# The front of a macaron block: loading all sequences of x at once, issuing the stores of x after those of the rows, and giving the experts' search its own SBUF places

## The chip, the core and the metric

The kernel runs on one core of a Trainium2 chip. The metric is the device time of one execution in microseconds (us). The median of three runs before the change is 5663.02 us (5660.18 to 5664.28). The profile is of one further execution.

Names used below: PE is TensorE's matmul, PEld its weight load, DVE is VectorE, ACT is ScalarE, POOL is GpSimd, SP is the engine whose queue issues most DMAs. L181 is line 181 of the kernel before the change.

## The reference, cut to what matters

The input x has 8 sequences of 1024 tokens of 256 float32 numbers. The network is two "layers": a half-weighted mixture of experts, causal attention, the same mixture again, then a channel mix, a state-space block and the channel mix again. Only the mixture bears on this change:

```python
def _L0_ffn_ref(x, Wr, br, W_up, b_up, W_down, b_down):
    ...
    k = n_tok // E                       # 8192 tokens, 8 experts: 1024 each
    xf = x.reshape(n_tok, h)
    logits = xf @ Wr + br
    Sm = jax.nn.softmax(logits, axis=-1)
    G_t, idx_t = jax.lax.top_k(Sm.T, k)  # each expert takes its 1024 best tokens
    ...
    y = jnp.zeros_like(xf).at[idx].add(G[..., None] * out)
...
x = L0_attn_x
x = x + 0.5 * _L0_ffn_ref(_layernorm(x, axis=-1), ...)
x = x + _L0_attn_ref(_layernorm(x, axis=-1), ...)
x = x + 0.5 * _L0_ffn_ref(_layernorm(x, axis=-1), ...)
```

An expert picks tokens among all 8192, so no expert can start before the probabilities of all eight sequences are known.

## The kernel before, in words

Nearly all data are float32, laid on 128 partitions. A sequence is a tile of 128 x 8 x 256: 8 pieces of 128 tokens. DRAM holds `acc` (x plus what is added to it) and `rows` (for each token its 256 normalised numbers and 8 probabilities). One SBUF tile `S` holds all probabilities.

**The front** (the loop at the start of `tile_macaron_kernel`, L1800 to L1804) does for each sequence b: load x into `xt` (L1802, 1024 KB, SP queue), `moe.front` (below), and store `xt` to `acc[0]` (L1804, 1024 KB, SP queue). The pool "f" has two buffers of each of its tiles, `xt` among them. Tile's scheduler orders the instructions of this loop itself: it is not under `tc.manual_schedule()`, within which each engine keeps the order in which the program wrote its instructions.

`steps_front` (L164 on) is a generator; `front` runs it through. For one sequence its steps are:

1. `normalise`: DVE takes the statistics (L75 x8, L77 x8), ACT the square root (L79), DVE the reciprocal (L81) and the normalised copy `moe_r` (L88 x8).
2. Four steps, each with four PE transposes (L177) of two pieces, and one ACT copy from PSUM into `moe_xT` (L181).
3. The logits: 16 matmuls, which the profile records as 32 with a weight load each (L186), and a DVE add of the bias (L191).
4. Maximum, subtraction (DVE, L196, L197) and exponential (ACT, L200).
5. Sum, reciprocal, product into `moe_r`, copy into `S` (DVE, L203 to L210), and the store of `moe_r` into `rows` (L213, 1056 KB, SP queue).

The square root and the exponential are in different ACT tables; a change between them puts an ACT_TABLE_LOAD ahead.

**The search** (`choose`, L217 on) transposes `S` (L227, L231), finds each expert's threshold in 30 rounds of DVE, PE, DVE (L249, L236, L254 to L262), and turns the chosen places into two tiles `lo` and `hi` (L300, L301). Its `full` tile is set by a POOL memset (L279).

**The experts** (`run`, under `tc.manual_schedule()`): POOL memsets of the weights' and middle tiles (L363 to L374), SP loads of the weights of the first two experts (`load(0)`, `load(1)`, L383 to L399), then the search in pools opened inside `run`, then for each expert a list of tokens (`steps_list`, L310 to L344), a gather of their rows (POOL, L428), the matmuls (L462, L479) and a scatter that adds into `acc` (POOL, L487).

`run` is called twice: after the front, and after the attention stage, whose own generator `steps_front` writes `S` and `rows[1]` (store at L908). Ahead of the second call, `Layer1` loads and prepares the weights of the second half (L1061 to L1116).

Of the kernel before, what the change touches and what calls it, by code (L numbers as in the profile page):

```python
# [8 lines left out]
F32 = mybir.dt.float32  # L9
# [5 lines left out]
PSUM = bass.MemoryType.PSUM  # L15
DRAM = bass.MemoryType.DRAM

P = 128
D = 256
# [3 lines left out]
E = 8  # L23
# [81 lines left out]
class Moe:  # L105
# [6 lines left out]
    def __init__(self, cp, net, Wr, br, W_up, b_up, W_down, b_down):  # L112
        self.net, nc = net, net.nc
        self.W_up, self.b_up, self.W_down, self.b_down = W_up, b_up, W_down, b_down
        C, KT = net.C, net.KT
        self.SC = C // self.SP
        assert self.SC * E == P
        self.wr = cp.tile([P, KC, E], F32, name="wr")
        nc.sync.dma_start(self.wr, Wr.rearrange("(k p) e -> p k e", p=P))
        self.br = cp.tile([P, E], F32, name="br")  # L120
        nc.sync.dma_start(self.br, br.partition_broadcast(P))

        one = cp.tile([P, E], F32, name="of_e")
        nc.vector.tensor_reduce(
            one, net.ident.rearrange("p (c e) -> p e c", e=E), AX.X, ALU.add
        )
        self.same = cp.tile([P, self.SC, E], F32, name="same")
        nc.vector.tensor_copy(self.same, one.unsqueeze(1).to_broadcast([P, self.SC, E]))
        self.same = self.same.rearrange("p c e -> p (c e)")
        self.before = cp.tile([P, P], F32, name="before")  # L130
        nc.gpsimd.affine_select(
            self.before, self.same, [[1, P]], ALU.is_gt, 0.0, base=0, channel_multiplier=-1
        )

        ii = cp.tile([P, P], I32, name="ii")
        nc.gpsimd.iota(ii, [[1, P]], base=0, channel_multiplier=0)
        self.col = cp.tile([P, P], F32, name="col")
        nc.vector.tensor_copy(self.col, ii)
        ip = cp.tile([P, 1], I32, name="ip")
        nc.gpsimd.iota(ip, [[0, 1]], base=0, channel_multiplier=1)  # L140
        self.row = cp.tile([P, 1], F32, name="row")
        nc.vector.tensor_copy(self.row, ip)
        ic = cp.tile([P, self.SP, self.SC], I32, name="ic")
        nc.gpsimd.iota(ic, [[1, self.SP], [self.SP, self.SC]], base=0, channel_multiplier=0)
        self.cno = cp.tile([P, self.SP, self.SC], F32, name="cno")
        nc.vector.tensor_copy(self.cno, ic)

        self.join = cp.tile([P, KT], F32, name="join")
        parts = net.ident.rearrange("p (g j) -> p j g", j=32)
        hi = cp.tile([P, KT], F32, name="join_hi")  # L150
        nc.vector.tensor_reduce(hi, parts[:, 0:KT, :], AX.X, ALU.add)
        nc.vector.tensor_reduce(self.join, parts[:, KT : 2 * KT, :], AX.X, ALU.add)
        nc.vector.scalar_tensor_tensor(self.join, hi, float(P), self.join, ALU.mult, ALU.add)
# [149 lines left out]
    def steps_list(self, e, lo, hi, wh, idx, two, ps):  # L303
# [39 lines left out]
        nc.tensor.matmul(pi, sums, self.join, start=True, stop=True)  # L343
        nc.vector.tensor_copy(idx, pi)  # L344

    def run(self, S, rows, acc):

        net, nc, tc = self.net, self.net.nc, self.net.tc
# [3 lines left out]
        with ExitStack() as st:  # L352
            def pool_in(name, bufs, **kw):
                return st.enter_context(tc.tile_pool(name=name, bufs=bufs, **kw))
# [4 lines left out]
            wp = pool_in("ex_w", 1)  # L359
# [17 lines left out]
            def load(e):  # L377
# [22 lines left out]

            load(0)
            load(1)
            lo, hi = (
                wp.tile([P, self.SP, self.SC, E], F32, name=name) for name in ("lo", "hi")
            )
            with tc.tile_pool(name="ch", bufs=1) as pool, tc.tile_pool(
                name="ch2", bufs=2
            ) as two, tc.tile_pool(name="ch_ps", bufs=2, space=PSUM) as ps:
                self.choose(S, lo, hi, pool, two, ps)
            tp, mp = pool_in("ex_t", 2 * KT), pool_in("ex_m", 2)  # L410
            op, ip, two = pool_in("ex_o", 4), pool_in("ex_i", 3), pool_in("ex_2", 2)
            pst, psm, pso = (
# [1328 lines left out]
def kernel(  # L1741
# [30 lines left out]
    nc = tc.nc  # L1772
    B, T, _ = x.shape
    net = Net(ctx, tc, B, T)
    N, NT = net.N, net.NT
# [3 lines left out]
    moe = Moe(mcp, net, Wr, br, W_up, b_up, W_down, b_down)  # L1779
    S = moe.probabilities(mcp)  # L1780
# [3 lines left out]
    acc = [dram1.tile([N, D], F32, name=f"acc{i}") for i in range(2)]  # L1784
    rows = [dram1.tile([N, ROW], F32, name=f"rows{i}") for i in range(2)]

    def of(a, b):

        return a[b * T : (b + 1) * T, :].rearrange("(c p) d -> p c d", p=P)

    def pool_in(st, name, bufs, **kw):
        return st.enter_context(tc.tile_pool(name=name, bufs=bufs, **kw))

    xf, of_out = x.rearrange("b t d -> (b t) d"), out.rearrange("b t d -> (b t) d")
    with ExitStack() as st:
        at = Attention(net, pool_in(st, "at_w", 1), w_qkv, w_out, b_out)
        with ExitStack() as ph:
            pool = pool_in(ph, "f", 2)
            ps = pool_in(ph, "f_ps", 3, space=PSUM)
            for b in range(B):  # L1800
                xt = pool.tile([P, NT, D], F32, name="xt")
                nc.sync.dma_start(xt, of(xf, b))  # L1802
                moe.front(pool, ps, xt, b, rows[0], S, "mm")
                nc.sync.dma_start(of(acc[0], b), xt)  # L1804
        with tc.manual_schedule():
            moe.run(S, rows[0], acc[0])
        with ExitStack() as ph:
            at.places(pool_in(ph, "at_qk", 1), dram1)
            pools = {
                name: pool_in(ph, f"at_{name}", bufs) for name, bufs in (  # L1810
                    ("x", 3), ("xn", 2), ("xT", 1), ("side", 1), ("pT", 4), ("so", 2), ("oT", 2),
                    ("over", 2), ("sm", 2), ("junk", 1), ("r", 1), ("rT", 1),
                )
            }
            for name, banks in (("s1", 3), ("s2", 3), ("po", 1), ("mm", 1)):
                pools[name] = pool_in(ph, f"at_{name}", banks, space=PSUM)

            pools["dram"] = dram2

            def load(xt, b):  # L1820
                nc.sync.dma_start(xt, of(acc[0], b))

            def store(xt, b):
                nc.sync.dma_start(of(acc[1], b), xt)
                yield from at.steps_front(moe, xt, b, rows[1], S)

            with tc.manual_schedule():
                at.run(pools, load, store)
    with ExitStack() as st:
        w = pool_in(st, "l1_w", 1)  # L1830
        layer1 = Layer1(
            net, w, Wr_t, Wk_t, Wv_t, mu_r, mu_k, ln_gamma, ln_beta, in_proj_t, conv_w, conv_b,
            x_proj_t, dt_proj_t, dt_proj_b, A_log, Dp, out_proj_t,
        )
        with tc.manual_schedule():
            moe.run(S, rows[1], acc[1])
        of_moe.close()
        pools = {
            name: pool_in(st, f"l1_{name}", bufs) for name, bufs in (
                ("x", 2), ("mixT", 1), ("ka", 2), ("r", 2), ("hT", 2), ("u", 1), ("uc", 2 * NDC),  # L1840
                ("xd", 1), ("delta", 1), ("du", 1), ("sp1", 1), ("zs", 1),
                ("rep", 1), ("sdl", 3), ("sdu", 3), ("dbu", 2), ("hc", 6), ("tap", 1), ("through", 1), ("xn", 2), ("small", 2),
            )
        }
        pools["dram"] = dram2
        pools["ps"] = pool_in(st, "l1_ps", 2, space=PSUM)
        pools["y"] = pool_in(st, "l1_y", 1, space=PSUM)
        pools["h"] = pool_in(st, "l1_h", 2, space=PSUM)

        def load(xt, b):  # L1850
            nc.sync.dma_start(xt, of(acc[1], b))

        def store(xt, b):
            nc.sync.dma_start(of(of_out, b), xt)

        def load_x(xt, b):
            nc.sync.dma_start(xt, of(acc[0], b))

        def keep_x(xt, b):
            nc.sync.dma_start(of(acc[0], b), xt)  # L1860

        with tc.manual_schedule():
            layer1.run(pools, load, load_x, keep_x, store)
# [39 lines left out]
```

## Time and profile before

| what | value |
|---|---|
| median of three runs | 5663.02 us |
| the profiled execution, its own time | 5670.78 us |
| its span, first to last instruction | 5668.9 us |
| PE busy | 4660.3 us (82%) |
| DVE busy | 3431.4 us (61%) |
| ACT busy | 2505.6 us (44%) |
| POOL busy | 2205.0 us (39%) |
| mean granted TensorE clock | 0.890 |
| last copy into S of the front begins | 129.05 us |
| first expert's list begins (L310) | 199.70 us |
| first expert matmul (L462, weight load) | 228.8 us |
| last copy into S ahead of the second search begins | 2294.17 us |
| second search begins (L227) | 2302.19 us |

In a row of the timeline stand: start, duration, engine, line, operation, tile written <- tiles read, shapes, how often, and in brackets how long its engine was idle before and what ended that. In a row of stretches stand: the stretch and its length, the busy time and number of instructions of PE, PEld, DVE, ACT and POOL, then the granted TensorE clock (1.00 is full), the mean busy share of the DMA engines, and the GB/s that they moved. SPq rows are DMAs as SP issues them. The profile has one execution; positions in it are us from the span's start.

### The profile page before, as it was taken

Reading aid. Unit: us, or ns where it says so; the run is one execution under the profiler, and the core shown is the slowest. Engines: PE = TensorE matmul, PEld = TensorE weight load, DVE = VectorE, ACT = ScalarE, POOL = GpSimd, SP = SyncE. Lnnn points to the kernel's source line nnn. Section 1 sums busy time; section 2 is a strip of 40 time slices with the busy share of each in tenths; the row PEclk is TensorE's granted clock in tenths of the full one; section 3 lists DMA queues with packets and bytes.
Section 4 is the critical chain, followed back from the end, with each engine's and each line's share of the span. In section 5 each row is a group of like instructions: output and inputs, shape, how many; then the busy total and the mean of one; then the engine's idle time right before and its main releaser. Section 6 shows DMA issues by size and latency. Waiting matters only on the chain.

```text
span 5668.9 us, 60303 instructions
## 1 busy us (share of the span) xinstructions
PE 4660.3 (82%) x21302; PEld 2227.0 (39%) x21302; DVE 3431.4 (61%) x5653; ACT 2505.6 (44%) x4152; POOL 2205.0 (39%) x1801
## 2 busy tenths in 40 slices
PE   5599699999999998399776778788787778878867
PEld 5355434444444443255532233333333324333324
DVE  4532166667666762633107877777767777677884
ACT  2011145666565553011144645465464645546443
POOL 1244201111111110234316656556555666556662
PEclk7699889999999997599887889889898888989888
DMA  6123312122221220223206454535536463454652
GB/s 201 33 57 60 79 37 75 58 74 68 81 74 59 77 69 27 68 49 62 44 13 156 134 145 122 153 98 143 138 105 158 110 163 108 112 153 114 169 137 63
DMA packets 252976, 545.28 MB, mean 96 GB/s; under 512 B 29681, under 2 KB 143681, under 8 KB 252674
## 3 DMA queue, kind: packets, MB, share of 16 engines
q1 hardware_dynamic: 228098, 507.34, 32.1%
q0 software_dynamic: 24576, 34.10, 3.7%
q8 instruction: 168, 2.75, 0.2%
q14 instruction: 134, 1.10, 0.1%
HBM read 400.31 MB, written 141.03 MB: 95 GB/s over the span
## 4 chain that ended last, share of the span: by engine, by line
PE 25%; DVE 13%; ACT 6%; issue 5%; DMA 2%; POOL 1%; SPq 0%; DVEq 0%; POOLq 0%; ACTq 0%
DVE h L1719 8%; PE y L1647 5%; PE pc L1366 4%; PE pr L1261 4%; PE pk L1239 4%; PE pu L1417 2%; DVE hc L1724 2%; PE pp L1501 2%; ACT h L1625 2%; PE pd L1432 1%; ACT xn L1195 1%; PE px L1396 1%; DMA sdu<-du 1%; DVE ln_st L1182 1%; ACT L1131 1%
## 5 line engine op out<-in xcount | busy, mean ns | idle before, releaser
L767 ACT ACTIVATE pT<-s 128x512 f32<-128x512 f32 (+3 forms) x1536 | 670.7, 488 | 554.9 <-PE s L724 546.7
L1625 ACT ACTIVATE h<-sdl,A 128x1024 f32<-128x1024 f32 x512 | 567.0, 1112 | 644.4 <-DVE hc L1724 622.4
L724 PE MATMUL s<-kT,qT 32*128 32x512 f32 (+3 forms) x3072 | 839.5, 540 | 12.9 <-DVE mx L740 8.0
L1647 PE MATMUL y<-hc,pick 128*32 128x512 f32 x2048 | 648.5, 714 | 227.6 <-DVE hc L1724 227.6
L724 PE MATMUL s<-qT,kT 32*128 32x512 f32 (+3 forms) x3072 | 763.7, 547 | 13.3 <-ACT pT L767 13.3
L1616 POOL TENSOR_TENSOR dbu<-sdu,b 128x1024 f32<-128x1024 f32 x256 | 602.3, 2353 | 405.3 <-DMA sdu<-du 217.5
L1719 DVE TENSOR_TENSOR_SCAN h<-h,dbu 128x1024 f32<-128x1024 f32 x256 | 586.1, 2289 | 184.4 <-ACT h L1625 159.8
L1719 DVE TENSOR_TENSOR_SCAN h<-h,sdu 128x1024 f32<-128x1024 f32 x256 | 586.2, 2290 | 160.6 <-ACT h L1625 146.3
L1724 DVE TENSOR_TENSOR hc<-h,c 128x1024 f32<-128x1024 f32 x512 | 625.6, 1222 | 30.4 <-PE y L1647 2.5
L773 POOL TENSOR_SCALAR_AFFINE_SELECT pT<-pT 128x512 f32<-128x512 f32 x256 | 162.4, 634 | 1180.7 <-ACT pT L767 1097.2
L1616 POOL TENSOR_TENSOR sdu<-sdu,b 128x1024 f32<-128x1024 f32 x256 | 602.4, 2353 | 14.4 <-DMA b<-bc 3.7
L724 PEld LDWEIGHTS s<-kT,qT 32*128 32x128 f32 x3072 | 327.6, 187 | 437.1 <-DVE mx L740 184.6
L466 ACT ACTIVATE mid<-pm,bu 128x512 f32<-128x512 f32 x192 | 131.6, 686 | 734.3 <-PE pm L462 734.3
L737 DVE TENSOR_REDUCE part<-s 128x1 f32<-128x512 f32 x512 | 329.7, 685 | 187.1 <-PE s L724 186.5
L487 POOL DMA_INDIRECT acc<-o,idx x128 | 211.2, 1650 | 502.0 <-DVE o L484 229.7
L1647 PEld LDWEIGHTS y<-hc,pick 128*32 128x32 f32 x2048 | 126.7, 125 | 712.0 <-issue 391.4
L740 DVE CUSTOM_DVE_ANT_0 junk<-s,mask,part 128x256 f32<-128x256 f32 (+3 forms) x512 | 281.5, 550 | 159.7 <-PE s L724 114.7
L462 PE MATMUL pm<-tT,wu 128*128 128x512 f32 x768 | 364.0, 612 | 0.0
L479 PE MATMUL po<-wd,mid 128*128 128x256 f32 x1536 | 352.0, 393 | 0.0
L787 PE MATMUL po<-pT,at_v 128*32 128x512 f32 (+3 forms) x3072 | 337.1, 512 | 0.3 <-POOL pT L773 0.3
L740 DVE CUSTOM_DVE_ANT_0 junk<-s,mask 128x256 f32<-128x256 f32 (+3 forms) x512 | 250.4, 489 | 136.5 <-PE s L724 84.9
L479 PEld LDWEIGHTS po<-wd,mid 128*128 128x128 f32 x1536 | 305.1, 200 | 44.3 <-issue 1.0
(262 smaller groups left out, 6736.8 us busy)
## 6 DMA issues: line engine op xcount, KB each, us to landing
sdl<-dl SPq DMA_DIRECT2D x256, 512.0 KB
sdu<-du SPq DMA_DIRECT2D x256, 512.0 KB
acc<-xt SPq DMA_DIRECT2D x24, 1024.0 KB
xt<-acc SPq DMA_DIRECT2D x24, 1024.0 KB
rows<-moe_r SPq DMA_DIRECT2D x16, 1056.0 KB
qT<-padded_q SPq DMA_DIRECT2D x32, 512.0 KB
kT<-padded_k SPq DMA_DIRECT2D x32, 512.0 KB
kept<-so SPq DMA_DIRECT2D x64, 256.0 KB
```

What stands on the lines that cost most here:

```text
L462: nc.tensor.matmul(pm, wu[:, k, n * P : (n + 1) * P], tT[:, k, t0 : t0 + HALF], start=(k == 0), stop=(k == KC - 1),)
L479: nc.tensor.matmul(po, mid[:, n, j * P : (j + 1) * P], wd[:, n, :], start=(n == 0), stop=(n == NF - 1),)
L724: self.net.nc.tensor.matmul(s[:, 0 : rhs.shape[-1]], lhsT, rhs, start=True, stop=True)
L737: nc.vector.tensor_reduce(part, sh, AX.X, ALU.max)
L740: nc.vector.tensor_tensor_reduce(junk[:, 0:w], sh[:, 0:w], self.mask[:, W - w : W], 1.0, part if a else -3e38, ALU.add, ALU.max, self.mx[n ...
L767: self.net.nc.scalar.activation(pT[:, h, 0:w], sh[:, 0:w], AF.Exp, scale=1.0 / HD**0.5)
L787: nc.tensor.matmul(q.po[h * HS : (h + 1) * HS, o:W], self.va[q.b % 2][:, j, g * HG + h, :], pT[:, h, 0 : W - o], start=(j == 0), stop=(j = ...
L1616: nc.gpsimd.tensor_tensor(inputs[i], t, seqs[b].rep["b", p], ALU.mult)
L1625: nc.scalar.activation(decays[i], spread["dl", i - p], AF.Exp, scale=self.A[:, p, n : n + 1])
L1647: nc.tensor.matmul(self.py[g * self.RG : (g + 1) * self.RG, t0 : t0 + W], self.pick[:, j, :], hc[:, t0 : t0 + W], start=False, stop=(j == ...
L1719: nc.vector.tensor_tensor_scan(decays[i], decays[i], inputs.pop(i), 0.0, ALU.mult, ALU.add)
L1724: nc.vector.tensor_tensor(hc, decays.pop(i), seqs[b].rep["c", p], ALU.mult)
```

## The change

There are four edits.

- Front: the eight tiles `xt` have a pool of their own with eight buffers, and all eight loads are issued first. The sequences are then worked through by a list of at most two generators of `steps_front`. A new one is admitted where the turn number is divisible by four and fewer than two are under way; in each turn every generator advances one step. With nine calls to a generator (eight steps and its end), sequence 0 starts in turn 0, sequence 1 in turn 4, sequence 2 in turn 12, sequence 3 in turn 16, and so on. When a generator ends, `xt` is stored to `acc[0]`, one turn after the store of its rows. All of it is under `tc.manual_schedule()`.
- `lo` and `hi` move from a pool of `run` to the pool of the experts' constants, which lies at the right side of SBUF.
- The search gets pools at the right side of SBUF (`room`), opened ahead of the front's pools, and a PSUM pool of its own (`chosen`).
- The search is called before `run` and not in it, for both layers; in `run`, loads and memsets are therefore behind it in the order of the program.

```diff
+        self.lo, self.hi = (
+            cp.tile([P, self.SP, self.SC, E], F32, name=name) for name in ("lo", "hi")
+        )
...
+    def room(self, st):
+
+        st = st.enter_context
+        return (
+            st(self.net.tc.tile_pool(name="ch", bufs=1, side="right")),
+            st(self.net.tc.tile_pool(name="ch2", bufs=2, side="right")),
+        )
+
+    def chosen(self, S, room):
+
+        with self.net.tc.tile_pool(name="ch_ps", bufs=2, space=PSUM) as ps:
+            self.choose(S, self.lo, self.hi, *room, ps)
...
             load(0)
             load(1)
-            lo, hi = (
-                wp.tile([P, self.SP, self.SC, E], F32, name=name) for name in ("lo", "hi")
-            )
-            with tc.tile_pool(name="ch", bufs=1) as pool, tc.tile_pool(
-                name="ch2", bufs=2
-            ) as two, tc.tile_pool(name="ch_ps", bufs=2, space=PSUM) as ps:
-                self.choose(S, lo, hi, pool, two, ps)
+            lo, hi = self.lo, self.hi
...
-        with ExitStack() as ph:
-            pool = pool_in(ph, "f", 2)
-            ps = pool_in(ph, "f_ps", 3, space=PSUM)
-            for b in range(B):
-                xt = pool.tile([P, NT, D], F32, name="xt")
-                nc.sync.dma_start(xt, of(xf, b))
-                moe.front(pool, ps, xt, b, rows[0], S, "mm")
-                nc.sync.dma_start(of(acc[0], b), xt)
+        with ExitStack() as ro:
+            room = moe.room(ro)
+            with ExitStack() as ph, tc.manual_schedule():
+                pool, px = pool_in(ph, "f", 2), pool_in(ph, "f_x", B)
+                ps = pool_in(ph, "f_ps", 3, space=PSUM)
+                xs = []
+                for b in range(B):
+                    xs.append(px.tile([P, NT, D], F32, name="xt"))
+                    nc.sync.dma_start(xs[b], of(xf, b))
+
+                todo, works = list(range(B)), []
+                turn = 0
+                while todo or works:
+                    if todo and len(works) < 2 and turn % 4 == 0:
+                        b = todo.pop(0)
+                        works.append((b, moe.steps_front(pool, ps, xs[b], b, rows[0], S, "mm")))
+                    turn += 1
+                    for b, steps in list(works):
+                        if next(steps, 0) == 0:
+                            works.remove((b, steps))
+                            nc.sync.dma_start(of(acc[0], b), xs[b])
+            with tc.manual_schedule():
+                moe.chosen(S, room)
         with tc.manual_schedule():
             moe.run(S, rows[0], acc[0])
...
         with tc.manual_schedule():
+            with ExitStack() as ro:
+                moe.chosen(S, moe.room(ro))
             moe.run(S, rows[1], acc[1])
```

## The prediction

> **What bounds the kernel here.** The page's chain of waits, asked for 0 to 700 us, has no piece there, so it does not say what the front is worth. I therefore read three stretches, cut where the trace changes its work: to the end of the last copy into S (129.05 + 0.20), to the first expert's list (199.70), to the first expert matmuls.
>
> ```profile
> 0.00:129.25 129.25, 77.22 (x384) 74.84 (x384) 59.87 (x265) 36.48 (x59) 10.92 (x22) 0.83 0.61 198
> 129.25:199.70 70.45, 21.53 (x74) 18.00 (x74) 43.81 (x170) 0.00 (x0) 8.68 (x11) 0.50 0.18 55
> 199.70:230.00 30.30, 12.48 (x150) 7.77 (x151) 25.34 (x31) 0.00 (x0) 13.79 (x11) 0.50 0.16 43
> ```
>
> In the front no engine is full: PE 77 of 129 us, DVE 60, ACT 36, DMA 0.61 of its time. It is bound by waits between them. The search (70.45 us) is a chain of DVE and PE in turn, and it starts from the last S. From 240 us on PE is busy 58.98 of 60 us. So a microsecond gained before the last S is gained one for one, and the change's other parts must be found between 129 and 230 us and at the second search.
>
> Next the timeline of the front, the rows that set its pace:
>
> ```profile
> 18.25 3.70 PE L177 MATMUL tr_moe<-ident,moe_r 128*128 128x128 f32 x16 [18.25 <-DVE moe_r L88]
> 21.74 6.84 PE L186 MATMUL moe_pl<-wr,moe_xT 128*128 128x8 f32 x32
> 28.43 3.85 PE L177 MATMUL tr_moe<-ident,moe_r 128*128 128x128 f32 x16
> 32.24 7.00 PE L186 MATMUL moe_pl<-wr,moe_xT 128*128 128x8 f32 x32
> ...
> 67.76 0.20 DVE L210 COPY S<-moe_r 128x64 f32<-128x64 f32 x1
> 67.87 2.71 DVE L75 BATCH_NORM_STATS2 ln_st<-xt 128x6 f32<-128x256 f32 x8
> ...
> 71.19 1.28 ACT L79 ACT_TABLE_LOAD   x1 [4.22 <-DVE ln_mv L77]
> ...
> 73.62 3.70 PE L177 MATMUL tr_moe<-ident,moe_r 128*128 128x128 f32 x16 [7.76 <-DVE moe_r L88]
> ...
> 77.11 4.12 PE L186 MATMUL moe_pl<-wr,moe_xT 128*128 128x8 f32 x32
> ```
>
> Sequences 0 and 1 form one PE block, 18.25 to 39.24 (20.99 us). The whole front is such blocks and gaps: blocks of 20.99, 20.24 (45.61 to 65.85), 7.61 (73.62 to 81.23), 21.04 (90.44 to 111.48) and 7.36 us (118.50 to 125.86), in sum 77.24; gaps between them of 6.37, 7.77, 9.21 and 7.02, in sum 30.37; 18.25 ahead and 3.39 behind. Sum 129.25, the measured end.
>
> Two rows stand out: the 32 logits instructions take 6.84 to 7.00 us in the blocks of two, but 4.12 (77.11) and 3.88 (121.98) in the lone ones. The stretches around them, cut every 3.41 us, show why:
>
> ```profile
> 74.68:78.09 3.41, 3.41 (x19) 3.41 (x17) 1.05 (x4) 2.34 (x4) 0.00 (x0) 1.00 1.03 322
> 78.09:81.50 3.41, 3.14 (x28) 3.04 (x27) 0.23 (x1) 0.00 (x0) 0.00 (x0) 1.00 1.04 335
> 81.50:84.90 3.40, 0.00 (x0) 0.00 (x0) 1.61 (x8) 2.79 (x3) 0.00 (x0) 0.50 0.03 8
> 119.08:122.49 3.41, 3.41 (x19) 3.41 (x17) 1.53 (x5) 2.02 (x4) 0.00 (x0) 0.50 0.54 179
> 122.49:125.90 3.41, 3.38 (x30) 3.29 (x30) 0.00 (x0) 0.33 (x1) 0.00 (x0) 1.00 0.00 0
> ```
>
> The clock goes from 0.50 to 1.00 at 122.49 and back at 125.90. (Up to the first fall at 81.5 the column says 1.00 throughout, but the durations show half clock; I go by the durations.) The step comes after a window that the 3.7 us of transposes fill wholly or mostly; 78.09 and 122.49 lie 13 x 3.415 us apart, so the windows seem to run on a fixed grid. At 18.25 or 90.44 the transposes straddle two windows, and the logits stay slow. So six sequences ran at half clock, two at full clock, and whether a sequence is lucky hangs on its start against a grid that this kernel doesn't set.
>
> **Loads at once.** Eight loads stand at the head of SP's queue; two of them took 1.06 us to issue, so six more take about 3.2 us of an SP that otherwise waits until 12 us. Sequence 0 landed at 12.19 (first statistics), sequence 1 at about 15.15 (SP's wait for it, the shorter of two, 2.6 us after 12.56): one after the other, 3.0 us apart. By this the last lands at 12.2 + 7 x 3.0 = 33 us, and is needed past 100. What goes: SP's waits at L1802, 18.3 us for the store of x and 14.0 for DVE. But they are not four times on the path, since what is late next is the chain of the pair itself.
>
> **The new order.** By the turns, sequences 0/1, 2/3, 4/5, 6/7 form pairs: the second starts with the first's last transposes, and the first of the next pair is written behind the S copy of the pair before. On DVE that is a strict order: S copy, then statistics. The trace has this handover at 65.85: logits end, S copy ends at 67.96, statistics at 67.87, table load, transposes at 73.62, a gap of 7.77 us. Inside a pair, the second's normalisation lies under the first's logits: in the pair at 18.25, DVE would end it by 17.3 + 2.7 + 2.7 + 0.6 + 0.6 + 2.7 = 26.6, before 28.43, so the block stays 21.0 us. The sum, all at half clock: first transposes at 18.09 (the reciprocal no longer stands behind six statistics of the next sequence, 17.15 for 17.31), four blocks of 21.02 = 84.06, three gaps of 7.77 = 23.31, and 2.11 behind the last logits (65.85 to 67.96; no table load, the pair's first exponential did it). That is 127.57, against 129.25: 1.7 us less.
>
> So the gaps fall by 7.06 us, the tail by 1.28 and the start by 0.16, but the blocks grow by 6.82, most of which is the two lucky sequences (6.95 - 4.12 and 6.95 - 3.88: 2.83 + 3.07 = 5.9). Bounds for luck: none of eight, or six or so of eight (2.4 us of transposes in one window were enough at 74.68, 2.2 us at 91.77 were not; so by an estimate from these, about 2 of the 3.41 us of the grid are lucky starts). I take two of eight as in this trace: 127.6 - 5.9 = 121.7, a gain of **7.5 us**. The lucky span is one window, so 2.9 us each.
>
> [...]
>
> **Stores.** A row store landed 4.8 us after issue (129.05; the wait at L383 ended 133.87). `moe_r` has two buffers; sequence 0's store goes out near 32.8 and its buffer is written again near 46.5, 13.7 us later, so nothing waits. Per pair of 28.8 us the stores are 4.3 MB, 150 GB/s where 12 to 18 us shows 368. The last x store is now behind the last rows: about 3 us more until the experts' weights and memsets may enter those places. They took 8.4 us (134.04 to 142.43) and are needed at 200.4 (wh) and 228.8 (wu), so 57 us of search hide them; uncovered they would cost those 8.4.
>
> **The search's places.** Before, the transposes of S began 0.11 us after the copy ended (129.36): no wait goes. At the second search PE's row at 2302.19 was released by ACT's A (L1115), whose chain begins with the load of A_log, issued at 2295.20 and landed at 2301.16. That stays. If the new places lie over `moe_r`, whose store was issued at 2294.16, the first write (2303.35) would wait for it; the DMAs were at 1.02 up to 2300 and at 0.19 after, so it had landed 3 us before. Zero. POOL's `full` (0.52 us) moves ahead of the memsets and is needed 60 us later: zero.
>
> **The sum** against the profiled execution: 5670.8 - 7.5 = 5663.3. The median of the runs is 7.8 us below that execution, so I put the same difference on it: 5663.0 - 7.5 = 5655.5.
>
> **Rivals.**
> - Forecast, one to three lucky sequences: -4.6 to -10.4, so 5652.6 to 5658.4. Chance 0.48.
> - The gaps shrink but no sequence is lucky: -1.7, 5661.3. For it: six of eight before were not. Chance 0.20. [...]
> - Four or more lucky: five give -1.7 - 14.7 = -16.4, 5646.6. The three table loads in the gaps could add 3 x 1.28 if they went out early, as the one at 83.65 did. For it: four pairs start after 7.8 idle us, as both lucky ones did. Chance 0.24.
> - Slower: the eight loads share the DMA engines evenly, and sequence 0 lands with the last at 33 us, not at 12.2. That is 20.8 later for the whole front: -7.5 + 20.8 = +13.3, 5676.3. It loses as soon as sequence 0 lands later than 19.7. Against it: sequences 0 and 1 landed 3 us apart though issued together. Chance 0.08.
>
> A measurement of this kernel can tell about 0.2%, 11.3 us, from no change. The first two cases lie within it (0.68), the third is faster (0.24), the fourth slower (0.08). The range reaches from six lucky ones and part of the table loads (-22) to the second case and a few us of shift further on (+4): 5641 to 5667; it leaves out the fourth case and the tail of the third.
>
> **What would show it.** Right: eight loads in a row on SP from 3.3; first transposes near 18.1 and, of the third sequence, near 46.9; three gaps near 7.8; the last S between 117 and 128; the list 70.4 us behind it. Wrong: sequence 0 not landed by 13; a PE wait inside a pair; a wait for a row store at L88; a second search later than 8 us behind its last S.

## The result, and the profile after

The changed kernel took 5650.92 us (median of 14 runs, 5634.01 to 5662.78) against 5662.1 us (14 runs, 5639.07 to 5671.88). The ratio is 0.9975 with a 95% interval of 0.9965 to 0.9985: 0.25% faster, about 14 us, 8 to 20 by the interval. The profiled execution took 5638.44 us with a span of 5636.2.

| position or length, us | before | after |
|---|---|---|
| first transposes of the front | 18.25 | 17.96 |
| last copy into S ends | 129.25 | 109.25 |
| first expert's list begins | 199.70 | 179.64 |
| search, last S to list | 70.45 | 70.39 |
| first expert matmul to first attention exponential | 527.2 | 519.2 |
| second search's first transpose behind its last S copy's start | 8.0 | 8.0 |
| span | 5668.9 | 5636.2 |

The same stretches as before the change (stretch, length, busy time of PE, PEld, DVE, ACT, POOL with counts, clock, DMA share, GB/s):

```profile
0.00:109.25 109.25, 65.51 (x384) 62.43 (x384) 62.14 (x265) 33.50 (x57) 11.33 (x23) 0.69 0.67 221
109.25:179.60 70.35, 21.48 (x74) 17.95 (x74) 43.77 (x170) 0.00 (x0) 8.21 (x10) 0.50 0.25 77
```

The front is 20 us shorter with the same 384 PE instructions. PE itself was busy 11.7 us less (65.51 for 77.22): less idle time is only part of it, the same instructions also ran faster. The search kept its length. The front's PE rows:

```profile
17.96 3.69 PE L180 MATMUL tr_moe<-ident,moe_r 128*128 128x128 f32 x16 [17.96 <-DVE moe_r L88]
21.44 3.73 PE L189 MATMUL moe_pl<-wr,moe_xT 128*128 128x8 f32 x32
25.03 3.59 PE L180 MATMUL tr_moe<-ident,moe_r 128*128 128x128 f32 x16
28.84 4.39 PE L189 MATMUL moe_pl<-wr,moe_xT 128*128 128x8 f32 x32 [0.23 <-ACT moe_xT L184]
...
63.52 3.69 PE L180 MATMUL tr_moe<-ident,moe_r 128*128 128x128 f32 x16 [7.77 <-DVE moe_r L88]
67.01 6.83 PE L189 MATMUL moe_pl<-wr,moe_xT 128*128 128x8 f32 x32
73.70 3.79 PE L180 MATMUL tr_moe<-ident,moe_r 128*128 128x128 f32 x16
77.56 6.99 PE L189 MATMUL moe_pl<-wr,moe_xT 128*128 128x8 f32 x32
92.33 3.69 PE L180 MATMUL tr_moe<-ident,moe_r 128*128 128x128 f32 x16 [7.77 <-DVE moe_r L88]
95.81 4.01 PE L189 MATMUL moe_pl<-wr,moe_xT 128*128 128x8 f32 x32
```

Six of the eight sequences have their 32 logits instructions in 3.7 to 4.4 us, the pair at 63.52 alone in 6.8 to 7.0. The gaps ahead of pairs are 7.71, 7.77 and 7.77 us (41.2 us of PE's waits for `moe_r` with the first one's 18.0). Cut along the grid of 3.413 us that the clock's steps give (here its falls at 24.91 and 106.83 lie 24 x 3.413 us apart):

```profile
18.09:21.50 3.41, 3.41 (x17) 3.33 (x18) 3.41 (x12) 1.76 (x3) 0.00 (x0) 1.00 1.10 348
21.50:24.92 3.42, 3.42 (x33) 3.42 (x33) 3.01 (x17) 0.89 (x2) 0.00 (x0) 1.00 1.10 348
24.92:28.33 3.41, 3.41 (x17) 3.18 (x17) 2.17 (x8) 2.14 (x4) 0.00 (x0) 0.50 1.11 350
28.33:31.74 3.41, 3.18 (x29) 2.94 (x27) 0.84 (x4) 1.43 (x3) 0.00 (x0) 1.00 1.09 347
...
62.46:65.87 3.41, 2.35 (x11) 2.30 (x12) 3.11 (x10) 1.14 (x3) 0.00 (x0) 0.50 0.89 298
65.87:69.29 3.42, 3.42 (x19) 3.42 (x17) 2.99 (x17) 1.73 (x4) 0.00 (x0) 0.50 0.02 5
```

PE is fully busy in each of the first three. After the window of transposes (18.09) the next is fast, with 33 instructions in it; after that window of logits the clock is 0.50 again. At 62.46 only 2.35 us are transposes, and the window after it stays at 0.50. (Up to the first fall, at 24.9 here, the column says 1.00 whatever the durations say.)

SP's rows, one execution of the changed kernel:

```profile
3.30 21.00 SPq L1815 DMA_DIRECT2D xt<-in_L_attn_x_dram  x8
...
109.05 0.36 SPq L216 DMA_DIRECT2D rows<-moe_r  x1
109.45 0.76 SPq L1827 DMA_DIRECT2D acc<-xt  x1
117.54 0.37 SPq L399 DMA_DIRECT2D wu<-in_L_ffn_W_up_dram  x1
```

The eight loads held SP for 21 us, and nothing was due on SP before 29.09. The experts' weights entered the front's places at 117.54, 8.3 us behind the last S.

### The profile page after: what moved, and what is told of

It reads as the page before. It is cut to its first block, busy times and chain, and to the rows that moved or that the text cites. A ratio compares the mean times of both kernels' runs of the same rounds, so it can differ in the third digit from the quotient of the medians.

```text
span 5636.2 us, 60291 instructions
## 1 busy us (share of the span) xinstructions
PE 4643.4 (82%) x21302; PEld 2203.4 (39%) x21302; DVE 3432.4 (61%) x5653; ACT 2503.6 (44%) x4150; POOL 2204.0 (39%) x1801
## 4 chain that ended last, share of the span: by engine, by line
PE 26%; DVE 13%; ACT 6%; issue 5%; DMA 2%; POOL 1%; SPq 0%; DVEq 0%; POOLq 0%; ACTq 0%
DVE h L1729 8%; PE y L1657 5%; PE pc L1376 4%; PE pr L1271 4%; PE pk L1249 4%; PE pu L1427 2%; DVE hc L1734 2%; PE pp L1511 2%; ACT h L1635 2%; PE pd L1442 1%; PE pm L472 1%; ACT xn L1205 1%; PE px L1406 1%; DMA sdu<-du 1%; PE po L489 1%
## 5 line engine op out<-in xcount | busy, mean ns | idle before, releaser
L476 ACT ACTIVATE mid<-pm,bu 128x512 f32<-128x512 f32 x192 | 131.6, 686 | 722.2 <-PE pm L472 722.2
```

## The experiments

The theory at their start (A): the new order of the pairs and the PE clock set the front's length, the early loads are cover. Rivals: the early loads are the gain (B); the search's places are (C); the fast logits have another cause than the transposes' windows (D). All kernels compute the whole reference.

**Loads first, alone.** The front of before, with:

```diff
-                xt = pool.tile([P, NT, D], F32, name="xt")
-                nc.sync.dma_start(xt, of(xf, b))
-                moe.front(pool, ps, xt, b, rows[0], S, "mm")
+                xs.append(px.tile([P, NT, D], F32, name="xt"))   # px: 8 buffers
+                nc.sync.dma_start(xs[b], of(xf, b))
+            for b in range(B):
+                moe.front(pool, ps, xs[b], b, rows[0], S, "mm")
```

> The front of before with the eight loads issued first into eight buffers; the order of the engines is still the scheduler's, the search and its places are as before. Theory A (the new order of the pairs and the PE clock set the front's length; the loads are cover): the last S stays between 120 and 132 us, the kernel within 0.1% of before. Rival B (the early loads are the gain, since SP no longer waits 32 us for buffers): the last S falls to 110 to 122 us and the kernel gains most of the 14 us. Rival C (the search's places): nothing changes here.

Measured: ratio 0.9983 (0.9970 to 0.9996) to before; last S at 122.9 us, with none of the eight sequences at full clock (32 logits in 6.83 to 7.00 us each where together). Before had two at full clock: at none it would stand at 129.25 + 5.9 = 135.1. So at equal clock the early loads are worth 12 us in the scheduler's own order. Theory A's "cover" falls here, although the 122.9 lies in its range. The kernel gains 9.6 us (2 to 17), most of the 14, as Rival B says; its last S was to be at 122 or less.

**The order, alone.** After, with two buffers of x, each load behind the store of the x two before:

```diff
-                pool, px = pool_in(ph, "f", 2), pool_in(ph, "f_x", B)
+                pool, px = pool_in(ph, "f", 2), pool_in(ph, "f_x", 2)
...
                             nc.sync.dma_start(of(acc[0], b), xs[b])
+                            fetch()        # the load of the next sequence
```

> After, but with two buffers of x: a sequence is loaded only when the x of the one two before it has been stored. Theory A: a pair's load comes late by the store's landing and the load itself, some 2 to 6 us in each of three gaps, so the gaps grow from 7.8 to 10 to 14 us and the last S comes 6 to 18 us later than in after; the kernel is within 0.2% of before. Rival B: the same sign, but the whole gain goes and the last S is at 129 us or later. Rival C: the gain of 14 us stays.

Measured: ratio 1.0030 (1.0018 to 1.0043), last S at 144.1 us, one sequence at full clock. The gaps ahead of pairs are 14.64, 12.87 and 12.92 us. From the waits by engine (what waited, us in total, times, longest):

```profile
DVE ln_st L75 <- DMA xt<-in_L_attn_x_dram: 35.3, 7, 8.8
```

Seven waits for x stand in the place of one of 8.7. The last S is 35 us later than in after, where Theory A expected 6 to 18: 17.2 us by the three gaps, 2.3 by a wait inside the second pair, and 15.5 by five sequences fewer at full clock. Rival B foresaw that the whole gain goes, and more did: the order alone is slower than before. The order needs the loads. The loads without the order kept 9.6 of the 14 us, and the two intervals overlap (0.9970 to 0.9996, 0.9965 to 0.9985), so the kernel times do not show what the order adds to the loads; in the profiles it brings the last S from 122.9 to 109.1 us.

**The places, alone.** The front of before, the search called ahead of `run` with its pools at the right, in both layers.

> The front of before, with the search called ahead of the experts and in places of its own, in both layers. Theory A: the search still begins 0.1 to 0.3 us behind the last S in the first layer and 8 us behind it in the second; the kernel is the same as before within 0.1%. Rival C: the search starts or runs faster and the kernel gains 5 to 14 us.

Measured: ratio 1.0020 (1.0005 to 1.0034). Last S at 131.6 us with one sequence at full clock, the search 0.3 us behind it, as before. No gain, so Rival C falls. The profile explains 2.5 us of the loss, by one sequence fewer at full clock; the rest of these 11 us (3 to 19 by the interval) stays open.

**The new front, without the places.** After's front, with the search inside `run` as before (the three other edits undone):

> The new front alone: eight loads first, pairs, stores of x behind rows, but the search called in the experts' run with its pools above the weights, as before. These pools (some 130 to 150 KB into a partition, by the sizes of the tiles) lie over the last of the eight tiles of x, whose store landed 8.3 us behind the last S in after. Theory A (the search's own places do not gain on before, but save a wait that the eight tiles bring): the last S stays as in after (104 to 127 us by luck), but the transposed S or the full tile waits for that store, and the search ends up to 8 us later than in after; in the second layer nothing changes; the kernel gains 0 to 0.2% on before. Rival C' (the places are of no use in either case): the search begins 0.3 us behind the last S and the kernel is as after.

Measured: ratio 1.0007 (0.9998 to 1.0017), last S at 115.3 us, four sequences at full clock. The start of its search:

```profile
115.30 0.20 DVE L210 COPY S<-moe_r 128x64 f32<-128x64 f32 x1
...
123.05 0.69 DVE L231 COPY ST<-pS 128x512 f32<-128x512 f32 x1 [7.56 <-DMA acc<-xt]
```

The pools of the search lie over the last x, and DVE waits 7.56 us for its store. The first list begins 76.7 us behind the end of the last S in place of 70.4. So the places gain nothing on the kernel before, and save 6.3 us on this front: eight tiles, and the store of x put behind that of the rows, would bring this wait. The list still begins 7.6 us earlier than before (192.15 for 199.70), and the runs show no gain; this stays open.

**Transposes and logits mixed.** After, with the logits of two pieces behind the transposes of the next two (and five PSUM buffers in the front):

```diff
             nc.scalar.copy(xT[:, :, c0 * P : (c0 + 2) * P], pt)
+            if c0:
+                logits(c0 - 2)
             yield
+        logits(NT - 2)
```

> After, with the logits of two pieces written behind the next pieces' transposes, so that no 3.41 us of PE are mostly transposes (about a third of each window at half clock, where 2.43 us were enough and 2.39 us were not); five PSUM buffers for the front in place of three. The same PE work in another order. Theory A (the full clock comes from a window with 2.4 us or more of transposes): no logits run at full clock, all take about 215 ns each, and the last S is at 127.6 us, within 2 us. Rival D (what made logits fast was something else of their time or neighbours, as DMA traffic): some sequences still run at 125 to 130 ns an instruction, and the last S is near 110 to 120 us.

Measured: ratio 1.0003 (0.9990 to 1.0017), last S at 125.1 us, no sequence at full clock. One sequence of it:

```profile
17.98 1.99 PE L190 MATMUL tr_moe<-ident,moe_r 128*128 128x128 f32 x8 [17.98 <-DVE moe_r L88]
19.79 1.88 PE L181 MATMUL moe_pl<-wr,moe_xT 128*128 128x8 f32 x8
21.52 1.09 PE L190 MATMUL tr_moe<-ident,moe_r 128*128 128x128 f32 x4
22.41 1.71 PE L181 MATMUL moe_pl<-wr,moe_xT 128*128 128x8 f32 x8
```

Eight logits instructions take 1.71 us, 214 ns each, wherever they stand, while loads and stores run beside them as in after (the DMA engines are 0.63 busy over its first 109 us, in after's front 0.67). Rival D falls (the count over all profiles, under the next heading, says the same). The last S is 2.5 us ahead of the 127.6 expected, since a pair's PE block takes 20.4 us here and not 21.0 (4 x 0.6). With this edit, the last S is 16.0 us later than in after, and all of the kernel's gain is gone (0.28%, 16 us), though the last S is still 4 us ahead of before's.

**Profiled again.** The changed kernel and the kernel before, both unaltered.

> The changed kernel unaltered, to see how much of the front is luck. Theory A: the number of sequences at full clock is another one (most likely 3 to 7 of 8), the last S is at 127.6 us less 2.4 to 2.9 us for each, and the three gaps stay at 7.7 to 7.8 us. Rival (the six of the first profile belong to the new order itself): six again, last S at 109 us within 1 us.

> The kernel before, unaltered, for a second look at its front. Theory A (its scheduler breaks some sequences' transposes up, so fewer of them fill a window): at most three of eight sequences at full clock, last S at 126 to 135 us. Rival (the number is luck alone, the same for both orders): four or more, last S at 123 us or less.

Measured: the changed kernel has six at full clock again (the first three pairs, where the first profile had all but the third), last S at 109.8. The kernel before has two again, last S at 128.6. Over the profiles, the new order with its loads had 6, 6, 4 and, in the run below, 6; the scheduler's order 2, 2, 1 (places alone) and 0 (loads alone). So which ones are fast is luck; how many is not only luck, as far as these eight profiles go, and the rival to "luck alone" holds.

Theory A's number came for the kernel before, but its reason, broken-up transposes, falls short. The order alone, above, has the 16 transposes of every sequence in one piece, and one sequence at full clock; the scheduler's order has them in one piece for seven of eight in both profiles of before, and two. The second profile of before has this sequence:

```profile
25.39 3.85 PE L177 MATMUL tr_moe<-ident,moe_r 128*128 128x128 f32 x16
29.20 7.00 PE L186 MATMUL moe_pl<-wr,moe_xT 128*128 128x8 f32 x32
```

A window of the grid runs from 24.76 to 28.17 there. Transposes take 2.79 us of it, and the next window is at 0.50. Counted over the fronts of all twelve profiles (the time of `tr_moe` in each window), full clock followed all 33 windows with 2.81 us or more of transposes, 4 of the 13 with 2.61 to 2.79, and none with less; nor did it follow any of the 64 windows that PE filled with logits and under 0.5 us of transposes. What decides between 2.61 and 2.79 is open.

So a sequence's start has to meet the grid, and the starts hang on one another. In after, a slow pair and the gap behind it take 28.81 us (63.52 to 92.33), 8.44 windows: the next pair stands at another place on the grid. It was fast behind all three such slow pairs (here, without the places, with A_log first). In before, 18.25 to 45.61 is 27.36 us, 8.02 windows: the same place, and slow again. In the order alone, 87.23 to 121.19 is 33.96 us, 9.95 windows: slow again. This fits the counts, but no run alters the gap alone, so it is argued and not shown.

The spans less the last S say how much the rest varies: 5527.1 and 5525.9 us in the two profiles of after, 5540.6 in the run below, whose experts are the same code; 5539.8 and 5534.8 in those of before. The first expert stage took 519.2, 525.2 and 527.8 us in these three. The 12.7 us by which after's first profile gained outside the front lie inside this.

**A_log first.** After, with the load and preparation of A_log at the head of `Layer1`:

> After, with the load and preparation of A_log written first in the second half's preparation, so that the second search no longer stands behind it. The places of the search lie over moe_r by the wait of the full tile's memset for the row store (5.2 us behind the last S in after). Theory A (the cover is then gone, and the search waits for that store): the second search begins 5.2 to 5.6 us behind the last S, in place of 8.7; the kernel gains 3 us on after. If the transposed S has a place beside moe_r, it begins 0.3 to 1 us behind it, and the gain is 8 us. If A_log's load cannot start earlier for want of its place, nothing changes. The kernel as a whole is 0.2 to 0.4% faster than before.

Measured: ratio 0.9966 (0.9953 to 0.9979); last S of the front at 109.2. At the second search, first after, then this kernel:

```profile
2273.46 0.52 POOL L282 MEMSET full<- 128x512 f32 x1 [23.29 <-DMA rows<-moe_r]
```

```profile
2278.18 0.20 DVE L915 COPY S<-moe_r 128x64 f32<-128x64 f32 x1
...
2283.18 0.69 DVE L234 COPY ST<-pS 128x512 f32<-128x512 f32 x1 [4.81 <-DMA rows<-moe_r]
```

The new places do lie over `moe_r`. In after its store lands 3.8 us before the transposed S is written (2277.22), because that waits for A_log (DVE waits 6.8 us for its load). With A_log out of the way the wait for the store shows: 5.0 us from S to ST in place of 9.2. In the runs this gain on after is not shown, as the two intervals overlap.

**Three under way, and the best found.** After with up to three sequences; then the same with A_log first and the second search's pools back at the left side.

```diff
-                pool, px = pool_in(ph, "f", 2), pool_in(ph, "f_x", B)
+                pool, px = pool_in(ph, "f", 3), pool_in(ph, "f_x", B)
...
-                    if todo and len(works) < 2 and turn % 4 == 0:
+                    if todo and len(works) < 3 and turn % 4 == 0:
```

> After, with up to three sequences under way (and three buffers of the front's tiles), so that a new one starts every four turns without a break. Theory A: the three gaps of 7.8 us close and PE runs through; the last S is at 18 + 8 x 10.5 + 2 = 104 us with no sequence at full clock and 87 to 104 with up to six; the kernel is 25 to 42 us faster than before. Rival B (loads and stores set the pace): the last S stays at 109 us or later, the kernel about as after.

> Three sequences under way, A_log first as in e5_alog, and the second search's pools back at the left side, so that they do not lie over moe_r. Theory A: last S at 90 to 110 us as with three alone, second search 0.3 to 1 us behind its last S; 8 us less than three sequences alone, so 25 to 45 us (0.45 to 0.8%) less than before.

Measured: three alone 0.9966 (0.9953 to 0.9980) to before, last S at 95.2 us, five at full clock; its gaps are at most 2.22 us. That is 19 us (11 to 27), less than the 25 to 42 expected, while the front did what was expected. The last one has the lowest ratio of all, 0.9946 (0.9928 to 0.9964), 31 us, within the 25 to 45 expected, though its interval overlaps with that of three alone: last S at 95.9, four at full clock, and the second search's ST 1.4 us behind its S:

```profile
2271.77 0.19 DVE L915 COPY S<-moe_r 128x64 f32<-128x64 f32 x1
...
2273.18 0.69 DVE L234 COPY ST<-pS 128x512 f32<-128x512 f32 x1 [1.21 <-PE pS L230]
```

## Why the prediction was right, and where a step of it failed

The measured median lies in the range (5641 to 5667), and the sign was right. The gain was larger than the forecast 7.5 us, and what the trace shows of the front is the third case, to which the prediction gave 0.24. Of the signs that the prediction named, the first transposes, the gaps and the 70.4 us came; the third sequence at 46.9 and the last S at 117 to 128 did not (40.94 and 109.1), because of the fast pairs. That the median lies in the range is in part luck: the range reached to six fast sequences, and the whole moved by less than the front.

- **What bounds the front: right.** The last S came 20.0 us earlier, the first list 20.1. The search kept its 70.4 us.
- **The sum at half clock: right.** First transposes 17.96 for 18.09, gaps 7.71 to 7.77 for 7.77, tail 2.1. By six fast sequences of 3.1 us each, the 109.1 stands for 127.6 at half clock; without any, the mixed kernel measured 125.1.
- **"I take two of eight as in this trace": this step failed.** It is a term of the sum that was mis-sized. The prediction had the rule from its trace (a window of 3.41 us with enough transposes), and an estimate by which about 2 of 3.41 us of the grid are lucky starts, some five of eight; then it took the count of the old order. But the old order is not a sample of the new one: its starts follow each other at other distances, and its scheduler breaks up the transposes of one sequence of eight (at 54 to 62 us, pieces of 1.09 and 2.16 us between logits). The profiles of the new front with its loads gave 4 to 6, about 3.1 us each: 12 to 19 us, not 5.9. The distances are the likelier reason, as worked out above, but argued; that the full clock is the gain, the mixed kernel shows.
- **"2.4 us of transposes in one window were enough": too low as a bound.** The prediction's own trace has a window with 2.46 us (102.01 to 105.42) that full clock did not follow; by the same count the window at 74.7 has 2.61. Over all profiles 2.81 were always enough, and 2.79 not always.
- **"The gaps shrink but no sequence is lucky": fell.** In after, six of eight had full clock, each behind a window with 2.65 us or more of transposes (18.08 to 21.50: 3.41 us). In the front of the mixed kernel, with 1.09 to 2.08 us of transposes in one piece, none had.
- **The loads: right as a sum, wrong on SP.** Sequence 0 landed as before (DVE's wait of 8.7 us both times), so the slower rival fell. But six more loads did not take 3.2 us of SP: the eight took 21.0, their median 2.92 us each, about a load's transfer (1.05 MB at the 348 GB/s of 12 to 18 us, 3.0 us). Free here, as SP's next DMA was due at 29.09. The prediction had no price for the loads without the new order; at equal clock the runs give 12 us.
- **The stores: right.** No wait for a row store. SP waited 4.2 us for the last rows and 2.8 more for the last x, where about 3 were expected.
- **The search's places: zero against before, which is right, and incomplete.** The prediction did not ask what the eight tiles and the late store would do to a search left in `run`: 7.56 us of wait, 6.3 of them net. The overlap with `moe_r` at the second search was there, hidden as it said.
- **One for one into the whole: not settled.** The front gained 19 to 20 us in three profiles; the runs show 14 (8 to 20). The runs are not profiled, so their number of fast sequences isn't known, and the rest varies by 15 us in these three profiles.

In one account at half clock, last S in us: before 135.1 (129.25 + 5.9), loads alone 122.9, order alone 147 (144.1 and one fast sequence), both 127.6. At equal clock the new order is 4.7 us worse than the scheduler's with the same loads; in these profiles it wins by six sequences at full clock against none. Whether it beats the loads alone in kernel time is not shown.

## What to carry to other kernels

When a sum has a term that depends on the PE clock, work the term out for the new order and don't copy the old order's count: how instructions are grouped, and where the groups start against the clock's windows, set it here (2.81 us of transposes inside one window of 3.413 us were always enough, 2.79 not always). When buffers are added or a store is moved back, ask what will be placed over them next, and when their last DMA lands. A part that gains nothing alone can be what keeps another part's gain, so undo parts from the changed kernel as well as adding them to the old one.

## What the runs showed of the hardware

- In these fronts PE's clock rose for one window of 3.413 us after every window with 2.81 us or more of 128x128 float32 transposes (33 of 33), after 4 of 13 with 2.61 to 2.79, and after none with less. A window in which PE was busy throughout with logits (128x128 weights, 8 columns moving) did not hold it: 21.50 to 24.92 at 1.00 was followed by 0.50. In one piece, the 32 logits instructions took 6.83 to 7.00 us at half clock and 3.72 to 4.78 at full clock.
- Eight loads of 1024 KB in a row held SP's queue for 21.0 us, where two took 1.06 us. Here nothing else was due on SP before their end (24.30), so no run shows what a later DMA would lose by it.
